# Reordering the first slot, the router and the POOL work of a fused attention + mixture-of-experts kernel

## The chip, the cores and the metric

One core of a Trainium2 chip runs the whole program. The metric is the device time of one execution in microseconds (us). An engine of the core is named as in the profile: PE does the matmuls and transposes, DVE the element-wise vector work, ACT the activation functions, POOL (GpSimd) some element-wise work and all DMAs whose rows are chosen by an index in memory ("indirect"), and SP issues the plain DMAs.

## The reference, cut to what matters

Everything is in 32-bit floats. B = 8 batches, S = 1024 tokens, D = 512; the attention has 16 heads of 32; the experts are E = 8, two per token, 512 to 2048 to 512, at most 160 tokens of a batch per expert.

```python
# attention: no projections; Q, K and V are sines and cosines of scaled inputs
xh = layernorm(x).reshape(B, S, 16, 32)
Q = concat(cos, sin)(xh / (1 + |w_q|) + b_q + t * phi_q)     # K alike
V = cos(.) + sin(.)   of  xh / (1 + |w_v|) + b_v
out = causal_softmax(Q @ K.T / 8) @ V
x = x + cos(.) + sin(.)   of  out / (1 + |w_out|) + b_out
# experts
xn2 = layernorm(x)
p, e = top_k(softmax(xn2 @ Wr + br), 2)
pos = place of the token within its expert, in this batch; kept if pos < 160
y = relu(xn2[rows of e] @ W1[e] + b1[e]) @ W2[e] + b2[e]
x = x + sum over the two experts of p * y
```

## The kernel before, in words

**Attention.** It runs as 32 slots, n = 0 to 31; slot n is batch b = n // 4 and a quarter c = n % 4 of the features (four heads, as two pairs). In a slot PE makes scores (`scores`, matmuls at L680), ACT takes their exponential (L700), PE multiplies by V (`attend`, L714), and PE turns the result (`turn`, through L215). Meanwhile the next slot's angles are made: `qk_pre` has PE transpose the input and DVE form `qk_f` (L521), `angle` makes `qk_r` or `t_r` (L440), ACT squares (L444) and takes sines, `v_pre` and `v_post` (L450) make V. The angle's part t * phi is a table per feature quarter, a "base": `make_base(c)` computes it once and stores it (`base_d`), and later batches load it (`load_base`). Bases 0 and 1 are made at the very start, 2 and 3 in slot 0, base 3 from a POOL iota (L463) through DVE (L471, L491, L225, L226) before `t_r` of the next slot.

**Router.** `router(b)` is a generator that the next batch's slots advance at places written out by hand. The slot c = 0 of batch b + 1 is followed by a "begin" slot (c = 1; the flag `begin`): there DVE makes second-layernorm rows (`rows`, L788), which SP stores to `xn2_d`, PE transposes two of them, DVE copies them out (`xT`, L815, or ACT at L807 for the last batch), PE makes logits (`sums`, L851). Later steps choose the two experts, count the places with PE (L834, from `prior`, L917 to L919), and leave 16 scatters, each of 128 (token, gate) pairs, to a table `slot_d[b]`. POOL issues them in `scatter` (L762); `fetch_slots` (L967) reads the table back to `meta`. `find_rows` (DVE) turns it into row numbers, with which `gather` (POOL DMA, then PE transposes at L215 or L1067) collects an expert's inputs.

**Experts.** For each expert two chunks, of six and four tiles of 128 rows. Both layers are Strassen products, seven matmul products in place of eight, so that weights and inputs have to be mixed (subtracted) first: `mix_w1` (L1095 to L1098, on POOL in the first chunk, else DVE) and `mix_w2` (DVE, L1020 to L1023). Layer 1 is eight steps q of seven products (L1111), layer 2 has a block of seven products (L1156), of eight matmuls each, per pair of tiles; a block ends with `gated` and two `send` (L1178), indirect DMAs that add rows to the output. The last batch's router has no later attention slots; `ending()` advances it, one step per product, through the first chunk's layer 1.

**What sets the order.** PE, DVE, ACT and SP issue in the order in which the program text reaches their instructions. POOL's order is chosen by a scheduler, but where the code pins an instruction. A pool of buffers makes an instruction wait until the former user of its buffer is done; DMAs that write the same table are ordered by waits unless the code says that they are independent.

Of the kernel before, what the change touches and what calls it, by code (L numbers as in the profile page):

```python
# [73 lines left out]
def preln_attn_moe_kernel(  # L74
# [421 lines left out]
    def load_base(n):  # L496
        if n == 2:
            rest(make_base(n))
        if n < NCH:
            return  # L500
        p = qkt.tile([P, 2, S], F32, name="qk_base")
        nc.sync.dma_start(p, base_d[n % NCH])
        bases[n] = p
# [253 lines left out]
    scatters = []  # L757

    def scatter():
        while scatters:  # L760
            b, idx, src = scatters.pop(0)
            nc.gpsimd.indirect_dma_start(  # L762
                out=slot_d[b], out_offset=bass.IndirectOffsetOnAxis(ap=idx, axis=0),
                in_=src, in_offset=None,
            )

    def router(b):
# [9 lines left out]
        for t in range(NTT):  # L777
            nc.vector.bn_aggr(mv[:, t, :], stats[:, t, :, :].rearrange("p c s -> p (c s)"))
        rstd = inverse_root(mv[:, :, 1], "rstd")

# [15 lines left out]

        last = b == B - 1

        def features(g):

            xT = row2.tile([P, NCH, 2 * P], F32, name="xT", bufs=1)
            if last:
                for i, xn in enumerate(ahead):
                    ps = pools["ps_tr"].tile([P, NCH, P], F32, name="ps_t")
                    for c in range(NCH):
                        nc.tensor.transpose(ps[:, c, :], xn[:, c * P : (c + 1) * P], ident)
                    copy(xT[:, :, i * P : (i + 1) * P], ps)  # L807
            else:
                ps = two_banks()
                for i, xn in enumerate(ahead):  # L810
                    for c in range(NCH):
                        at = (NCH * i + c) * 64
                        by_halves(ps[:, :, at : at + 64], xn[:, c * P : (c + 1) * P])
                for a in range(2):
                    copy(  # L815
                        xT.rearrange("p c (i a q) -> p i c a q", a=2, q=64)[:, :, :, a, :],
                        ps[:, a, :].rearrange("p (i c q) -> p i c q", i=2, q=64),
                    )
            if g + 1 < NTT // 2:
                ahead[:] = [rows(2 * g + 2), rows(2 * g + 3)]  # L820
                if not last and 2 * g + 4 == NTT:
                    store()
            return xT

# [42 lines left out]
        for g in range(NTT // 2):  # L867
            xT = features(g)
            yield
            lg = sums(g, xT, lg)  # L870
            yield
# [89 lines left out]
    def fetch_slots(b):  # L961

        rows = slot_d[b][: E * CAP, :].rearrange("(e c) k -> c e k", e=E)
        s0 = b * CAP
        while s0 < (b + 1) * CAP:
            s1 = min((s0 // P + 1) * P, (b + 1) * CAP)
            nc.gpsimd.dma_start(  # L967
                meta[s0 % P : s0 % P + s1 - s0, :, s0 // P, :],
                rows[s0 - b * CAP : s1 - b * CAP],
            )  # L970
            s0 = s1
# [72 lines left out]
    def gather(i):  # L1044

        e, j0, nh = chunks[i]
        xe = pools["xep"].tile([P, NCH, 2, HALF], F32, name="xe")
        for j in range(2 * nh):
            xg = pools["gp"].tile([P, D], F32, name="xg")
            nc.gpsimd.indirect_dma_start(  # L1050
                out=xg, out_offset=None, in_=xn2_d[i % 2],
                in_offset=bass.IndirectOffsetOnAxis(ap=source[:, e, j0 + j, None], axis=0),
            )
            yield None
            dst = xe[:, :, j // nh, j % nh * P : (j % nh + 1) * P]
# [23 lines left out]

    def start(gen, box):  # L1080
        for box[0] in gen:
            yield
# [4 lines left out]
    def mix_w1(i, q):  # L1087
        w = w1_tiles.pop((i, q))
        t = pools["t1p"].tile([P, 4, 2, P], F32, name="t1")
        b11, b12 = w[:, :2, 0, :], w[:, :2, 1, :]  # L1090
        b21, b22 = w[:, 2:, 0, :], w[:, 2:, 1, :]
        t1, t2, t3, t4 = (t[:, k, :, :] for k in range(4))

        mix = nc.gpsimd.tensor_tensor if i == 0 else TT
        mix(t1, b12, b11, ALU.subtract)  # L1095
        mix(t2, b22, t1, ALU.subtract)  # L1096
        mix(t3, b22, b12, ALU.subtract)
        mix(t4, b21, t2, ALU.subtract)  # L1098
        t1_tiles[i, q] = b11, b21, b22, t1, t2, t3, t4
# [47 lines left out]
    def layer2(i, block, hs, aside):  # L1147
# [29 lines left out]
        def send(r):  # L1177
            nc.gpsimd.indirect_dma_start(  # L1178
# [3 lines left out]
            )  # L1182

# [5 lines left out]
        TT(u2, p1, product(5, 4), ALU.add)  # L1189
        TT(u3, u2, product(6, 5), ALU.add)  # L1190
        p5 = product(4, 3)
        TT(u2, u2, p5, ALU.add)
        TT(u2, u2, p3, ALU.add)
        gated(0, 1, u2)
        send(0)
# [16 lines left out]
    def experts_begin():  # L1212

        for name, bufs in (("w1p", 3), ("t1p", 2), ("xep", 1), ("tmp_p", 2), ("gp", 2)):
            pools[name] = to_end.pool(name, bufs, **right)
        find_rows(0)
        for k in range(AHEAD):
            load_ahead(k)
        yield from start(gather(0), first_parts)
        mix_w1(0, 0)  # L1220

    def experts(ending):
        pools["hp"] = to_end.pool("hp", NHQ, **right)
        pools["ps_tr"] = to_end.pool("ps_tr", 2, space=PSUM)
        pools["ps_p"] = to_end.pool("ps_p", 6, space=PSUM)
        box = first_parts
        mixes = loads = iter(())
        for i, (e, j0, nh) in enumerate(chunks):
            parts, box = box[0], [None]
            hs = []  # L1230
            for q in range(NHQ):
                load_ahead(i * NHQ + q + AHEAD)
# [3 lines left out]
                if q > 1:  # L1236
                    next(mixes, None)
                hs.append(layer1(i, q, parts, [ending]))
                if i == 0 and q == NHQ // 2:
                    rest(ending)  # L1240
                    to_router.close()
                    for name, bufs in (("w2p", NHQ), ("yp", 3), ("bp", 1)):
                        pools[name] = to_end.pool(name, bufs, reuse_waits="tile", **left)
                    load_b2(0)
                    rest(load_w2(0))
                elif i == 0 and q == NHQ - 2:
                    mixes = mix_w2(0)
                    next(mixes)
            rest(mixes)
            aside = start(gather(i + 1), box) if i + 1 < len(chunks) else iter(())  # L1250
            for block in range(nh):
                if i == 0 and block == 1:
                    find_rows(1)
                layer2(i, block, hs, aside if i or block else iter(()))
# [24 lines left out]
    load_x(1)  # L1279
    v_post(0, v_st)  # L1280
    magnitude(inv_o)
    rest(base1)
# [3 lines left out]
    place, angles, residual = [None], iter(()), iter(())  # L1286
    for n in range(NCK):
# [5 lines left out]
        pos_n = trig.tile([P, S], F32, name="o_p")  # L1293
        if late:
# [34 lines left out]
        if n == 0:  # L1329
            with_asides(2)  # L1330
        if n == 0 or begin:

            qk_st = rest(qk_pre(n + 1))
            angle(*qk_st)
            angles = keep(place, both(qk_st))
            if n == 0:
                rest(make_base(3))
# [4 lines left out]
        route_on(1)  # L1342
        route_on(1)
# [8 lines left out]
        for g in asides:  # L1352
            rest(g)
        if late:
            turn(1, halves1, pos)
            o_st = o_pre(n - 1, pos)
        route_on(1)
        if n == 2:
            load_b1()
        if c == 3 and b > 0:  # L1360
# [3 lines left out]
            scatter()  # L1364
# [13 lines left out]
        if n == 0:  # L1378
            load_base(2)

# [18 lines left out]
        elif n + 2 < NCK:  # L1399
            qk_st = rest(qk_pre(n + 2))  # L1400
# [3 lines left out]
        route_on(1)  # L1404
# [8 lines left out]
        if more:  # L1413
# [18 lines left out]
    def ending():  # L1432

        o_st = o_pre(NCK - 1, pos_n)
        yield
# [4 lines left out]
        rest(o_post(NCK - 1, o_st))  # L1440
        for _ in range(3):
            yield
        for name in router(B - 1):

            for _ in range(5 if name == "tiles" else 1):
                yield
        fetch_slots(B - 2)
        scatter()
# [34 lines left out]
```

## Time and profile before

| | us |
|---|---|
| median of 3 runs | 3327.51 (3321.74 to 3332.6) |
| the profiled execution | 3319.22 |
| its span, first to last instruction | 3317.5 |
| PE busy | 3195.8 (96%) |
| DVE busy | 2260.7 (68%) |
| ACT busy | 1321.3 (40%) |
| POOL busy | 427.6 (13%) |
| mean granted PE clock | 0.994 |

Attention fills the span from about 40 to 1300 us, some 38.6 us a slot; the experts follow from 1301.7 to about 3306. "Busy" is the time in which an engine works; a share is of the span, over stages of different kinds. A line of the timeline gives the start, the length, the engine, the line of the kernel, the operation with its output and inputs, how many instructions it groups, and in brackets how long the engine sat idle before it and what ended that. A line of the waits gives the engine, the tile and line that waited, what it waited for, and then the total, the number of times and the longest, in us. Releasers are inferred.

### The profile page before, as it was taken

The page shows a single profiled execution, that of the slowest core. Times are in us where ns is not written, and L with a number is a line of the kernel's source. Part 1 is how long each engine was busy: PE and PEld are TensorE (multiplying, and loading weights), DVE is VectorE, ACT ScalarE, POOL GpSimd, SP SyncE. Part 2 cuts the span into 40 slices and gives each one's busy share as a digit, 9 for nine tenths or more (in the row PEclk, how much of TensorE's full clock was granted, in tenths as well). Part 3 has the DMA queues.
Part 4 walks back from the last instruction along what each step waited for, and adds up shares of the span by engine and source line. Part 5 has one row for each costly group of instructions (what it writes and reads, how often), then busy time and mean ns, then how long its engine had stood idle before and what let it go on. Part 6 is the DMA issues. An engine that isn't in the chain of part 4 may idle for free.

```text
span 3317.5 us, 48746 instructions
## 1 busy us (share of the span) xinstructions
PE 3195.8 (96%) x18942; PEld 2166.4 (65%) x18942; DVE 2260.7 (68%) x4953; ACT 1321.3 (40%) x1617; POOL 427.6 (13%) x395
## 2 busy tenths in 40 slices
PE   4999999999999998899999999999999999999998
PEld 2444444444444444588688688688688688688687
DVE  7787888878787675645845845845845845845854
ACT  6888888878787874201201201201201201201201
POOL 2000202021111203321011011011011011011010
PEclk9999999999999999999999999999999999999999
DMA  4445354544535343322322322422322322322321
GB/s 151 124 117 166 97 164 132 152 130 132 179 103 153 92 144 91 112 45 64 118 39 63 117 45 58 119 44 58 120 43 60 118 47 58 117 45 64 111 40 25
DMA packets 235254, 319.74 MB, mean 96 GB/s; under 512 B 22456, under 2 KB 155280, under 8 KB 222992
## 3 DMA queue, kind: packets, MB, share of 16 engines
q1 hardware_dynamic: 211664, 273.38, 27.8%
q0 software_dynamic: 22912, 43.22, 7.3%
q8 instruction: 150, 2.46, 0.3%
q14 instruction: 80, 0.66, 0.1%
q10 hardware_dynamic: 448, 0.02, 0.0%
HBM read 187.62 MB, written 61.82 MB: 75 GB/s over the span
## 4 chain that ended last, share of the span: by engine, by line
PE 56%; DVE 3%; DMA 2%; issue 1%; POOL 0%; ACT 0%; SPq 0%; POOLq 0%; DVEq 0%; ACTq 0%
PE ps_p L1156 28%; PE ps_p L1111 26%; DMA slot_d<-token,slot 1%; PE ps_t L1067 1%; PE ps_s L680 0%; PE av L714 0%; DMA out_dram<-y,slots 0%; DMA xg<-xn_d,source 0%; DVE t L1096 0%; DVE t L1095 0%; ACT hid L1143 0%; DVE hid L1139 0%; DVE u L1137 0%; DVE hid L1140 0%; DVE u L1132 0%
## 5 line engine op out<-in xcount | busy, mean ns | idle before, releaser
L700 ACT ACTIVATE e<-ps_s 128x1024 f32<-128x1024 f32 (+1 forms) x640 | 568.3, 938 | 214.3 <-PE ps_s L680 126.9
L680 PE MATMUL ps_s<-qk 64*128 64x512 f32 (+3 forms) x3072 | 599.5, 507 | 50.6 <-DVE qk_f L521 16.7
L1156 PE MATMUL ps_p<-w,hid 128*128 128x256 f32 x2560 | 569.8, 380 | 0.0
L1156 PEld LDWEIGHTS ps_p<-w,hid 128*128 128x128 f32 x2560 | 484.7, 190 | 66.5
L714 PE MATMUL av<-e,v 128*64 128x512 f32 (+3 forms) x3072 | 524.1, 490 | 0.0
L1156 PE MATMUL ps_p<-w_t,hid 128*128 128x256 f32 x1920 | 430.3, 379 | 0.7 <-DVE w_t L1022 0.7
L680 PEld LDWEIGHTS ps_s<-qk 64*128 64x128 f32 x3072 | 263.0, 189 | 237.4 <-issue 108.6
L1156 PEld LDWEIGHTS ps_p<-w_t,hid 128*128 128x128 f32 x1920 | 361.8, 190 | 48.7 <-DVE w_t L1022 1.1
L714 PEld LDWEIGHTS av<-e,v 128*64 128x64 f32 x3072 | 200.6, 137 | 283.7 <-issue 267.6
L1111 PE MATMUL ps_p<-xe_s,t 128*128 128x256 f32 (+1 forms) x1024 | 299.1, 435 | 7.9 <-POOL t L1096 4.5
L1111 PE MATMUL ps_p<-xe,w 128*128 128x256 f32 (+1 forms) x1024 | 299.9, 436 | 1.4 <-issue 1.1
L1111 PE MATMUL ps_p<-xe,t 128*128 128x256 f32 (+1 forms) x1024 | 296.8, 433 | 0.0
L762 POOL DMA_INDIRECT slot_d<-token,slot x128 | 160.6, 1255 | 1044.7 <-issue 644.3
L1185 ACT COPY p<-ps_p 128x256 f32<-128x256 f32 x40 | 14.7, 368 | 612.1 <-PE ps_p L1156 612.1
L1111 PEld LDWEIGHTS ps_p<-xe_s,t 128*128 128x128 f32 x1024 | 194.1, 190 | 92.5 <-DVE t L1096 7.9
L1111 PEld LDWEIGHTS ps_p<-xe,w 128*128 128x128 f32 x1024 | 193.5, 191 | 84.3 <-DVE hid L1129 5.7
L1111 PEld LDWEIGHTS ps_p<-xe,t 128*128 128x128 f32 x1024 | 194.4, 190 | 80.9 <-issue 0.4
L1050 POOL DMA_INDIRECT xg<-xn_d,source x80 | 78.1, 977 | 1109.3 <-PE ps_t L1067 1024.2
L1178 POOL DMA_INDIRECT out_dram<-y,slots x80 | 126.4, 1580 | 662.3 <-DVE y L1173 522.9
L1126 ACT ACTIVATE p<-ps_p,b_t 128x256 f32<-128x256 f32 (+1 forms) x128 | 65.4, 511 | 329.9 <-DVE y L1172 169.7
L1130 ACT ACTIVATE hid<-hid 128x256 f32<-128x256 f32 (+1 forms) x128 | 60.1, 470 | 321.1 <-DVE hid L1129 321.1
L1143 ACT ACTIVATE hid<-hid,b_more 128x256 f32<-128x256 f32 (+1 forms) x128 | 71.8, 561 | 269.7 <-DVE hid L1142 269.7
(223 smaller groups left out, 3822.7 us busy)
## 6 DMA issues: line engine op xcount, KB each, us to landing
w<-in_L_ffn_W_dram SPq DMA_DIRECT2D x256, 256.0 KB
w<-in_L_ffn_W_dram SPq DMA_DIRECT2D x64, 512.0 KB
qk<-qk_c SPq DMA_DIRECT2D x124, 256.0 KB
qk<-qk_r SPq DMA_DIRECT2D x124, 256.0 KB
qk_base<-base_d SPq DMA_DIRECT2D x28, 1024.0 KB
xn_d<-xn SPq DMA_DIRECT2D x72, 256.0 KB
x_mid<-in_L_attn_x_dram SPq DMA_DIRECT2D x16, 1024.0 KB
out_dram<-x_mid SPq DMA_DIRECT2D x8, 2048.0 KB
```

The costliest lines, as they stand in the source:

```text
L680: nc.tensor.matmul(ps[:, a, at : at + w], lhsT=pair[r, 1, kb * P : (kb + 1) * P], rhs=pair[r, 0, q0 : q0 + w], start=at == 0, stop=not own ...
L700: nc.scalar.activation(e, ps[:, :, :n], AF.Exp, scale=UNIT * UNIT / math.sqrt(2 * DH))
L714: nc.tensor.matmul(av[a * 64 : (a + 1) * 64, q0 - 512 * h :], lhsT=vt[:, kb, 2 * pr + a, :], rhs=es[i][:, a, at : at + w], start=kb == 0, ...
L762: nc.gpsimd.indirect_dma_start(out=slot_d[b], out_offset=bass.IndirectOffsetOnAxis(ap=idx, axis=0), in_=src, in_offset=None,)
L1050: nc.gpsimd.indirect_dma_start(out=xg, out_offset=None, in_=xn2_d[i % 2], in_offset=bass.IndirectOffsetOnAxis(ap=source[:, e, j0 + j, None ...
L1067: nc.tensor.transpose(ps[:, c, :], xg[:, c * P : (c + 1) * P], ident)
L1111: nc.tensor.matmul(ps, lhsT=weights[:, k, :], rhs=rows[:, k, :], start=k == 0, stop=k == 1)
L1126: nc.scalar.activation(p1, product(b11, a11), AF.Identity, bias=b1_t[:, e * NHC + q : e * NHC + q + 1])
L1130: nc.scalar.activation(h11, h11, AF.Relu)
L1143: nc.scalar.activation(h12, h12, AF.Relu, bias=more)
L1156: nc.tensor.matmul(ps, lhsT=hs[k][:, part, cols], rhs=ws[k][weight], start=k == 0, stop=k == NHQ - 1,)
L1178: nc.gpsimd.indirect_dma_start(out=out, out_offset=bass.IndirectOffsetOnAxis(ap=meta[:, e, jj[r], 0:1], axis=0), in_=ys[r], in_offset=None ...
```

## The change

It has seven parts.

1. **First slot.** Base 1 is finished before V of slot 0, base 2 and the small `magnitude(inv_o)` move within slot 0, and base 3 is made in slot 1, not in slot 0.
2. **Begin slots.** On DVE, `v_post` and the next two rows come after `xT` and `qk_f`; later `xT` comes before `qk_f`.
3. **First gathers.** The first chunk's rows are found and four of its gathers issued in slot 30, into buffers of the router, and two more before the first mixtures.
4. **Scatters.** In the last two batches (6 and 7) they no longer wait for each other; half of batch 6's come behind the W1 mixture of q = 2 and the rest after it. The fetch of the slots waits for all scatters of its batch. Other batches stay as they are.
5. **First expert chunk.** The last router's steps come later, its places wait five products; W1's mixtures of q = 6 and 7 go to DVE; W2's mixtures are made 2, 3 and 3 at a time; `find_rows(1)` and the second chunk's gathers come earlier. POOL's order is pinned for the mixtures, the sends of the first chunk and the gathers of chunks 1 and 2.
6. **Layer 2.** Product (4, 3) comes before (6, 5), with it `send(0)`. This holds for all 40 blocks.
7. **Pools** of the expert part wait by tile when a buffer is reused (`reuse_waits="tile"`), and the `gp` pool comes first.

```diff
     def load_base(n):
-        if n == 2:
+        if n < NCH:
             rest(make_base(n))
-        if n < NCH:
             return
...
-    def scatter():
-        while scatters:
+    scattered = {b: [] for b in range(B)}
+    mixed = []
+    def scatter(count=2 * NTT * TOPK, together=False):
+        for _ in range(min(count, len(scatters))):
             b, idx, src = scatters.pop(0)
...
+            if together:
+                tc.add_manual_dep(
+                    ins, mixed[-1].name,
...
+                    reason="behind the mixture",
+                )
+                for other in scattered[b]:
+                    tc.declare_no_dep(ins, other, reason="rows of their own")
+            scattered[b].append(ins)
...
-            if g + 1 < NTT // 2:
-                ahead[:] = [rows(2 * g + 2), rows(2 * g + 3)]
-                if not last and 2 * g + 4 == NTT:
-                    store()
             return xT
+        def next_rows(g):
+            ahead[:] = [rows(2 * g + 2), rows(2 * g + 3)]
+            if not last and 2 * g + 4 == NTT:
+                store()
...
             xT = features(g)
+            if g + 1 < NTT // 2:
+                if not last:
+                    yield
+                next_rows(g)
             yield
...
-            nc.gpsimd.dma_start(
+            ins = nc.gpsimd.dma_start(
...
+            for other in scattered[b]:
+                tc.add_manual_dep(
...
+                    reason="rows of all scatters",
...
     def gather(i):
+        if i == 0:
+            t = row2.tile([P, NCH, 2 * P], F32, name="xT", bufs=1).rearrange("p c t -> p (c t)")
+            places = [row2.tile([P, D], F32, name="xn2") for _ in range(2)]
+            places += [t[:, :D], t[:, D:]]
+            there = [fetch(xg, j) for j, xg in enumerate(places)]
             yield None
+            there += [fetch_next(j) for j in (4, 5)]
...
-        mix = nc.gpsimd.tensor_tensor if i == 0 else TT
...
+        apart = i == 0 and q < 6
+        mix = nc.gpsimd.tensor_tensor if apart else TT
...
         TT(u2, p1, product(5, 4), ALU.add)
+        p5 = product(4, 3)
+        TT(p1, u2, p5, ALU.add)
+        TT(p1, p1, p3, ALU.add)
+        gated(0, 1, p1)
+        send(0)
         TT(u3, u2, product(6, 5), ALU.add)
-        p5 = product(4, 3)
-        TT(u2, u2, p5, ALU.add)
-        TT(u2, u2, p3, ALU.add)
-        gated(0, 1, u2)
-        send(0)
...
-        for name, bufs in (("w1p", 3), ("t1p", 2), ("xep", 1), ("tmp_p", 2), ("gp", 2)):
-            pools[name] = to_end.pool(name, bufs, **right)
-        find_rows(0)
+        for name, bufs in (("gp", 2), ("w1p", 3), ("t1p", 2), ("xep", 1), ("tmp_p", 2)):
+            pools[name] = to_end.pool(name, bufs, reuse_waits="tile", **right)
...
-        pools["ps_tr"] = to_end.pool("ps_tr", 2, space=PSUM)
-        pools["ps_p"] = to_end.pool("ps_p", 6, space=PSUM)
+        pools["ps_tr"] = to_end.pool("ps_tr", 2, space=PSUM, reuse_waits="tile")
+        pools["ps_p"] = to_end.pool("ps_p", 6, space=PSUM, reuse_waits="tile")
...
                 if q > 1:
-                    next(mixes, None)
+                    for _ in range(1 if i else 3):
+                        next(mixes, None)
...
                     mixes = mix_w2(0)
-                    next(mixes)
+                    for _ in range(2):
+                        next(mixes)
+            if i == 0:
+                find_rows(1)
             rest(mixes)
             aside = start(gather(i + 1), box) if i + 1 < len(chunks) else iter(())
+            if i == 0:
+                aside = behind(2, aside)
             for block in range(nh):
-                if i == 0 and block == 1:
-                    find_rows(1)
-                layer2(i, block, hs, aside if i or block else iter(()))
+                layer2(i, block, hs, aside)
...
-    v_post(0, v_st)
-    magnitude(inv_o)
-    rest(base1)
+    rest(base1)
+    v_post(0, v_st)
...
+        if n == NCK - 2:
+            find_rows(0)
+            next(first_gather)
...
             qk_st = rest(qk_pre(n + 1))
+            if begin:
+                v_post(n, v_st)
+                next(route)
             angle(*qk_st)
             angles = keep(place, both(qk_st))
-            if n == 0:
-                rest(make_base(3))
...
+        if n == 0:
+            load_base(2)
+            magnitude(inv_o)
...
-            scatter()
+            if b < B - 1:
+                scatter()
...
     def ending():
         o_st = o_pre(NCK - 1, pos_n)
+        scatter(NTT * TOPK // 2, together=True)
         yield
...
         for name in router(B - 1):
-            for _ in range(5 if name == "tiles" else 1):
+            if name == "tiles":
+                scatter(together=True)
+            for _ in range({"tiles": 6, "places": 5}.get(name, 1)):
                 yield
         fetch_slots(B - 2)
-        scatter()
+        scatter(together=True)
         fetch_slots(B - 1)
```

## The prediction

> **What bounds it now.** I read the page, then TensorE (PE) busy by stage, PE's waits, the timeline around each, and the chain of waits. PE is busy 3195.8 of 3317.5 us, so about 122 us are to be had. Windows (start:end, length, PE, PE weight loads, VectorE = DVE, ScalarE = ACT, GpSimd = POOL, clock, DMA share, GB/s):
>
> ```profile
> 0.00:40.00 40.00, 7.91 (x44) 4.86 (x46) 34.60 (x74) 26.21 (x28) 22.30 (x52) 1.00 0.60 171
> 40.00:80.00 40.00, 24.89 (x166) 12.14 (x163) 23.69 (x24) 24.03 (x24) 1.84 (x1) 0.83 0.42 135
> 160.00:1300.00 1140.00, 1102.44 (x9674) 544.03 (x9670) 886.44 (x1784) 923.12 (x932) 160.04 (x137) 1.00 0.46 133
> 1300.00:1400.00 100.00, 86.22 (x318) 50.88 (x319) 69.20 (x173) 27.20 (x48) 36.54 (x44) 0.97 0.40 124
> 1600.00:3200.00 1600.00, 1597.32 (x6769) 1260.28 (x6768) 1007.83 (x2352) 219.44 (x442) 161.90 (x126) 1.00 0.28 72
> ```
>
> The experts, half the time, lose 2.7 us in 1600 and DVE works 63% of it: nothing to win there. The loss sits at the start (15 us in 40–80), in the attention and in the first expert chunk (14 us in 1300–1400). PE's waits name it:
>
> ```profile
> PE ps_s L680 <- DVE qk_f L521: 16.7, 8, 4.0
> PE ps_s L680 <- ACT e L700: 13.5, 5, 10.9
> PE ps_s L851 <- DVE xT L815: 6.6, 8, 0.8
> PE ps_s L680 <- DVE xT L815: 4.5, 6, 0.9
> PE ps_p L1111 <- POOL t L1096: 4.5, 2, 3.7
> PE ps_t L1067 <- DMA xg<-xn_d,source: 3.6, 1, 3.6
> PE ps_t L834 <- DVE prior L917: 3.5, 1, 3.5
> ```
>
> The timelines give the places: the 10.9 us wait and what DVE does before it, one begin slot (the slot that starts a router), the tail.
>
> ```profile
> 53.32 1.54 DVE L471 TENSOR_SCALAR x_mid<-x_mid,vecs 128x1024 f32<-128x1024 f32 x2 [4.84 <-POOL x_mid L463]
> 47.27 4.27 PE L680 MATMUL ps_s<-qk 64*128 64x512 f32 x12 [4.01 <-DVE qk_f L521]
> 62.52 1.86 PE L680 MATMUL ps_s<-qk 64*128 64x384 f32 x6 [10.88 <-ACT e L700]
> 394.69 1.14 PE L680 MATMUL ps_s<-qk 64*128 64x384 f32 x8 [0.86 <-DVE xT L815]
> 399.13 1.99 PE L680 MATMUL ps_s<-qk 64*128 64x512 f32 x8 [2.62 <-DVE qk_f L521]
> 3309.85 1.55 POOL L1178 DMA_INDIRECT out_dram<-y,slots  x1 [4.00 <-DMA out_dram<-y,slots]
> ```
>
> The chain shows the scatters, each waiting until the one before has landed, with W1's mixture behind them:
>
> ```profile
> 1320.79 4.06 DMA slot_d<-token,slot
> 1325.11 4.69 DMA slot_d<-token,slot
> 1330.85 0.83 POOL slots L967
> 1331.70 0.74 POOL t L1095
> ...
> 1333.83 2.93 PE ps_p L1111 x4
> ```
>
> **What the skill says.** "DMA: Bandwidth & Descriptors", section "Anatomy of one DMA — SWDGE (gpsimd) path": about 2.0 us per DMA are fixed, nearly all completion latency. The trace agrees (shortest scatter landing 2.1 us, median 3.1), and POOL is busy only 0.96 us per scatter, so waiting, not issuing, is what side by side removes. The same page, "Two DMAs through the same engine are not ordered": only the completion semaphore orders them; so the slot fetch must wait for all 16. "TensorE: Matmul & The Clock Gate", "What's actually happening": after an idle window of some 3.4 us the array runs at half speed for about as long. Here twelve matmuls took 4.27 us after 4.01 idle, eight 2.06 just before it, and 40–80 was granted 0.83; so a long wait costs more than its length. "GPSIMD Engine Reference", "Specifications": POOL shares SBUF interfaces with two-input DVE instructions; L1144 took 1.76 us at 1391.7 against 0.56, with a POOL mixture beside it.
>
> **Part 1, first slot.** Before, slot 0's DVE runs v_post and base 1's tail, then qk_f (44.5), waits 4.84 us for POOL's iota, builds base 3 (1.54+1.23+1.23+2.29 = 6.29 us), and only then makes t_r at 59.6, which ACT's square (60.4) and three exponentials ahead of PE's 62.5 stand behind. After, base 3 is built in slot 1 and qk_f comes first: qk_f at 40.6 (2.72) and qk_r (1.23) end at 44.6; ACT's squares and absolutes (2.19+1.99) run to 48.7, v_p's and t_r's DVE work (1.28+1.22+0.69) meanwhile, v_p's square (1.15) to 49.8. So the exponentials start at about 49.8 instead of 61.5: 11.7 us, the 4.01 us wait at qk_f being inside it; a 2.64 us wait at 82.5 for o_p goes too, 14.3. But base 3's 6.29 us now stand before slot 1's t_r, ready about 3.3 us after ACT wants it; with ACT's slack about 2.65 is given back. Net about **11.7** (7 if both moved bases stall slot 1; 15 with none and the clock back). SP's queue gets the base stores before and after the qk sends in another order; the 1 MB stores delay nothing that is due within 20 us.
>
> **Part 2, begin slots (seven).** The waits sum to 26.0 us: 0.5–0.9 at xT, 1.6–2.6 at qk_f, 0.8 at the second xT. The diff puts av_sb, xT, qk_f ahead of v_post (1.21) and of the two rows (1.06, plus 0.55–0.83 waiting for xn2's store). So qk_f ends about 3.1 us earlier, and that wait goes. But v_post and rows still have to be done before the second xT, and DVE is without a pause from the first rows to it: 13.7–14.0 us before, 13.05 after, only the store wait being saved. What PE wins at qk_f it mostly waits for at the logits (L851). I take 1.0 per slot, +0.4 at the second xT: 1.4 × 7 = **10** (20 if PE has other work there; 26 would be all; 5 if v_post, now later, delays the next attend).
>
> **Part 3, gathers ahead (slot 31).** Waits of 2.76 (put down to the first mixture on POOL, which gathers queue with) and 0.69+1.88 (gathers): 5.3. Four gathers are issued a slot earlier (landing 3.4 us against 38.6 us), two more before the mixtures. Their price on POOL, 6 × 0.98, moves, it isn't added; queued behind them are batch 6's scatters. With about 1.2 us of half clock: **6.5** (4–8).
>
> **Part 4, chunk 0.** From 1301.7 to the end of its layer 2 PE works 154.6 us at full clock and takes 178: 23.5 lost. Before: 3.67 (mixture behind 16 chained scatters, 1278–1329), 1.69+1.90 (router's rows and copies), 3.52+0.93 (prior), 0.85, 0.69, 3.57 (chunk 1's gather behind batch 7's chain, 1366.7–1418.9 = 52 us), about 5 at half clock. After: 8 of batch 6's scatters stand before W1 mixture 2 (of q=2) and 8 behind it, at 0.96+0.3 each 20 us for a batch; mixture 3 is ready 32.6 us after the start, wanted at 39. The router begins two products later and waits five for its places, so the prior's stall is covered; but DVE has 52 us of work up to q=4's end, a bubble of 2.9 at the start, and 3.4 of waits on ACT: I take 57±2 us against PE's ideal 52.6 and 69.8 before: 13. W2's mixtures at 2+3+3 in q=6 and 7 take away 0.69, the earlier find_rows and gathers 3.57 and 1.7 of clock; against it 2.1 as DVE runs three mixtures (5.4 us) before (0,7)'s results, and 0.8 for a gather behind send(0). Batch 7's slots land 29.5 us after q=4, find_rows is reached at 34: if they are late, DVE, in order, stops, and layer 2 with it. Sum **18** (10–23.5). The fetch's new wait on all scatters has only POOL's mixtures and scatters behind it.
>
> **Part 5.** (4,3) before (6,5) brings send(0) forward by one product, 3.46 us. Elsewhere hidden; in the last block send(1), ready at 3307.0, starts at 3309.85 because send(0) lands late: it would start at 3307.3, **2.5** (0–3). Chunk 2's last gather is pinned behind a send: **−0.8**. Pools that wait by tile: nothing; the stage has 2.7 us of waits in all, and if a bank's release became later that is the rival below.
>
> Sum 11.7+10+6.5+18+2.5−0.8 = 47.9. The profiled execution took 3319.22 (span 3317.5 and 1.7 around it); 3271.3 after, a ratio of 0.9856. The median of the runs, 3327.51, is 0.25% above that execution; the ratio on it gives **3279.5**.
>
> **Rivals.** (a) Everything named goes: 15+20+8+23.5+3 = 69.5, 3258. For it: PE's order is untouched, and every removed wait has a late engine with time elsewhere (DVE 68%). Against: DVE's unbroken 13 us in the begin slots. (b) Given back: DVE is the limit there and in chunk 0's router (69.2 of 100 busy, with PE waiting on it at L806 and L834); lower ends 7+5+4+10+0−0.8 = 25, 3302. (c) Slower: in layer 2's new order DVE's last reading of (4,3) still waits for (6,5), now the later product, so (4,3)'s bank is held one product longer; with six banks there are five others to go on. If PE had to wait for it once a block, up to 3.46 us × 40 blocks = 138 us; at 1.2 us a block (47.9/40) the gain is gone, above it the kernel is slower: at 2 us, 3359. Against it: DVE at 63%, and its adds of 0.42 us each follow within a product. (d) The scatters side by side don't help: if landings under W2's and the output's traffic stretch (one took 8.2 us), chunk 0 keeps its 18: 3297, within (b).
>
> **How the numbers follow.** Forecast 0.62, (a) 0.13, (b) with (d) 0.18, nothing within 0.3% (10 us, about what a measurement can tell from no change) 0.03, (c) 0.04. Range 3256 to 3304: from (a) to (b), all but some 0.15. Forecast's own: 3268 to 3292. Faster 0.93, same 0.03, slower 0.04.
>
> **What would show it.** Part 1: the x6 at 62.52 comes 11 us earlier, and 80–120 has about as much PE time as before. Part 2: L680's wait on qk_f falls from 16.7 to under 3, L851's on xT rises from 6.6 to over 10. Part 3: no L215 wait on xg. Part 4: L1111 no longer waits on L1095/L1096, 1300–1400 shows over 92 busy, scatters of the last two batches stand under 1.4 us apart. Part 5: send(1) issued within 0.5 us of its data. Wrong if 1600–3200 shows over 10 us idle, or find_rows stalls DVE for microseconds.

## The result and the profile after

The changed kernel takes 3285.68 us (median of 4 runs, 3283.79 to 3287.43), the kernel before 3325.78 (4 runs, 3321.74 to 3332.6): a ratio of 0.9881 with a 95% interval of 0.9865 to 0.9897. The forecast was 3279.5 with a range of 3256 to 3304. The profiled execution of the changed kernel took 3283.79, with a span of 3282.1, so between the two profiled executions the gain is 35.4 us, where 47.9 had been summed up.

PE by stage, in the columns of the prediction. The stages are now at other places of the program, so only the first and the long one compare directly: 40 to 80 gained 8.9 us of PE time, 1600 to 3200 is as full as it was. The part numbers from here on are those of the prediction: its part 4 takes in parts 4 and 5 of the change, its part 5 is the change's parts 6 and 7 and the pinned gathers of chunk 2.

```profile
40.00:80.00 40.00, 33.83 (x249) 17.05 (x247) 26.27 (x30) 30.91 (x31) 2.13 (x1) 0.91 0.53 162
160.00:1300.00 1140.00, 1113.42 (x9682) 552.57 (x9680) 898.33 (x1826) 923.86 (x936) 169.47 (x148) 1.00 0.47 133
1300.00:1400.00 100.00, 92.68 (x376) 63.70 (x373) 70.92 (x172) 19.46 (x36) 34.08 (x37) 0.95 0.41 108
1600.00:3200.00 1600.00, 1596.74 (x6814) 1269.14 (x6813) 998.35 (x2355) 218.02 (x442) 165.16 (x128) 1.00 0.29 72
```

PE's waits of the changed kernel (total, times, longest). Against the list before: L680's wait on qk_f, now L679, fell from 16.7 to 3.9, and the waits for POOL's mixtures and for DVE's prior all but went. New in this size are small waits at lg and prob, and one of 4.7 us at the first matmul of layer 2 (L1214).

```profile
PE ps_s L679 <- ACT e L699: 10.5, 4, 5.9
PE ps_s L869 <- DVE xT L832: 5.5, 7, 0.8
PE ps_p L1214 <- DVE hid L1187: 4.7, 1, 4.7
PE ps_s L679 <- DVE prob L876: 4.0, 7, 0.6
PE ps_s L679 <- DVE qk_f L520: 3.9, 7, 0.6
PE ps_s L852 <- DVE lg L874: 3.5, 7, 0.6
PE ps_t L1117 <- DMA xg<-xn_d,source: 3.3, 2, 1.8
```

To see where the time went, take the start of the same matmul in both traces: the first score of a slot, the first layer-1 matmul of a step, and so on. Both kernels reach these places in the same sequence, so the difference at each is the gain so far.

| PE reaches | before, us | after, us | gain | gain of the stretch | predicted |
|---|---|---|---|---|---|
| slot 3 | 166.08 | 155.53 | 10.55 | 10.55 | 11.7 (part 1) |
| slot 30 | 1214.30 | 1193.98 | 20.32 | 9.77 | 10 (part 2) |
| layer 1, chunk 0 | 1301.69 | 1273.49 | 28.21 | 7.89 | 6.5 (part 3) |
| chunk 0, step q = 5 | 1371.46 | 1334.71 | 36.75 | 8.54 | 13 (of part 4) |
| layer 2, chunk 0, third block | 1456.18 | 1420.81 | 35.37 | -1.38 | 5 (rest of part 4; its terms add up to 3.1) |
| layer 1, chunk 2 | 1580.82 | 1547.50 | 33.32 | -2.05 | -0.8 |
| last matmul of layer 2 | 3305.34 | 3272.49 | 32.84 | -0.48 | 0 |
| end | 3317.5 | 3282.06 | 35.44 | 2.60 | 2.5 (part 5) |

Parts 1 to 3 and the tail came near to what was summed. That parts 1 to 3 give exactly the 28.2 forecast for them together is luck: they were off by -1.2, -0.2 and +1.4. The first chunk gave 7.2 instead of 18. These are its places in the changed kernel's timeline, with those of the first slots and of one begin slot:

```profile
52.31 2.08 PE L679 MATMUL ps_s<-qk 64*128 64x384 f32 x8 [5.93 <-ACT e L699]
93.12 1.14 PE L679 MATMUL ps_s<-qk 64*128 64x384 f32 x8 [2.88 <-ACT e L699]
385.26 1.99 PE L679 MATMUL ps_s<-qk 64*128 64x512 f32 x8 [0.56 <-DVE qk_f L520]
392.19 0.31 PE L852 MATMUL ps_s<-gather_e,lg 128*32 128x8 f32 x16 [0.57 <-DVE lg L874]
393.29 0.64 PE L869 MATMUL ps_s<-xT,wr_sb 128*32 128x256 f32 x8 [0.79 <-DVE xT L832]
1299.23 0.87 PE L869 MATMUL ps_t<-xT,wr_sb 128*32 128x256 f32 x8 [2.66 <-ACT xT L824]
1366.73 8.49 PE L1214 MATMUL ps_p<-w,hid 128*128 128x256 f32 x28 [4.66 <-DVE hid L1187]
1396.17 0.63 PE L1117 MATMUL ps_t<-ident,xg 128*128 128x128 f32 x4 [1.50 <-DMA xg<-xn_d,source]
```

The line at 1366.73 is the most expensive. DVE's timeline ahead of it shows why: after the last result of q = 6 five of W2's mixtures, of four instructions each, run one behind the other from 1357.57 to 1366.1, and only then the first result of q = 7 is read. PE's next product waits until then for a free bank, a part of the memory that it writes results to.

```profile
1357.09 0.56 DVE L1202 TENSOR_TENSOR hid<-hid 128x384 f32<-128x384 f32 x1 [0.68 <-ACT hid L1201]
1357.57 0.42 DVE L1050 TENSOR_TENSOR w_t<-w 128x256 f32<-128x256 f32 x1
...
1365.79 0.43 DVE L1053 TENSOR_TENSOR w_t<-w,w_t 128x256 f32<-128x256 f32 x1
1366.13 0.55 DVE L1187 TENSOR_TENSOR hid<-p,ps_p 128x384 f32<-128x384 f32 x1
```

### The profile page after: what moved, and what is told of

It reads as the page before. It is cut to its first block, busy times and chain, and to the rows that moved or that the text cites. A ratio compares the mean times of both kernels' runs of the same rounds, so it can differ in the third digit from the quotient of the medians.

```text
span 3282.1 us, 48761 instructions
## 1 busy us (share of the span) xinstructions
PE 3191.8 (97%) x18942; PEld 2166.0 (66%) x18942; DVE 2252.1 (69%) x4961; ACT 1322.4 (40%) x1617; POOL 421.3 (13%) x387
## 4 chain that ended last, share of the span: by engine, by line
PE 73%; DVE 6%; issue 3%; ACT 1%; DMA 1%; SPq 0%; POOL 0%; POOLq 0%; DVEq 0%; ACTq 0%
PE ps_p L1214 28%; PE ps_p L1169 25%; PE av L713 9%; PE ps_s L679 8%; ACT e L699 1%; PE ps_t L1117 1%; PE ps_s L215 1%; DVE qk_f L520 1%; PE ps_s L693 1%; DVE t L1153 1%; DMA xg<-xn_d,source 1%; DVE qk_r L450 0%; DMA xn_d<-xn 0%; DVE xT L832 0%; DMA qk<-qk_r 0%
## 5 line engine op out<-in xcount | busy, mean ns | idle before, releaser
L679 PE MATMUL ps_s<-qk 64*128 64x512 f32 (+3 forms) x3072 | 596.5, 505 | 32.8 <-DMA qk<-qk_r 12.4
L1214 PE MATMUL ps_p<-w,hid 128*128 128x256 f32 x2560 | 570.3, 380 | 4.7 <-DVE hid L1187 4.7
L1214 PEld LDWEIGHTS ps_p<-w,hid 128*128 128x128 f32 x2560 | 485.0, 191 | 71.6 <-DVE hid L1187 5.3
L1214 PE MATMUL ps_p<-w_t,hid 128*128 128x256 f32 x1920 | 428.9, 379 | 0.0
L679 PEld LDWEIGHTS ps_s<-qk 64*128 64x128 f32 x3072 | 262.4, 188 | 219.1 <-issue 106.9
L1214 PEld LDWEIGHTS ps_p<-w_t,hid 128*128 128x128 f32 x1920 | 362.0, 190 | 47.6
```

The source lines that it names most:

```text
L679: nc.tensor.matmul(ps[:, a, at : at + w], lhsT=pair[r, 1, kb * P : (kb + 1) * P], rhs=pair[r, 0, q0 : q0 + w], start=at == 0, stop=not own ...
L1214: nc.tensor.matmul(ps, lhsT=hs[k][:, part, cols], rhs=ws[k][weight], start=k == 0, stop=k == NHQ - 1,)
```

## The experiments

Each kernel is timed against the kernel before on the same chip; the changed kernel's own ratio, taken again in the second set, is 0.9888 (0.9871 to 0.9905). A ratio says what a whole kernel is worth; which stretch an edit moved is read from the trace, as in the table above. The changed kernel's two traces differ by 0.6 us in the first expert chunk and by up to 1.0 elsewhere, so less than that is no difference. Each set of four ran on one chip, the three sets on three different chips.

### W2's mixtures at 1, 1 and 6 again

```diff
-                    for _ in range(1 if i else 3):
-                        next(mixes, None)
+                    next(mixes, None)
...
-                    for _ in range(2):
-                        next(mixes)
+                    next(mixes)
```

> The changed kernel with W2's mixtures of the first chunk at 1, 1 and 6 again instead of 2, 3 and 3. Theory A (DVE is the limit at the switch from layer 1 to layer 2, so their place only decides where PE waits): the 4.7 us wait for a PSUM bank at the first layer-2 product goes and that product starts about 7 us earlier, but the fourth product, the first that needs all mixtures, waits some 6 to 8 us for six mixtures behind the row finding; its start and the end of the kernel move by less than 3 us. Theory B (the five mixtures in front of the last layer-1 results are themselves the loss): 5 to 7 us faster.

3294.79 us, 0.9906 (0.9877 to 0.9935). From the start of layer 1 to the third block of layer 2 it took 144.2 us (1283.85 to 1428.03), the changed kernel 147.3 (1273.49 to 1420.81). This stretch is "the first chunk" in what follows. Of the 3.2 us less, 0.9 come before q = 5, where the two are the same. The whole isn't faster, because slots 30 and 31 took 8.6 us longer here; that is taken up with the changed kernel's second run. The wait of 4.7 us is gone, and the one that theory A had put at the fourth product came out as 0.27:

```profile
1372.66 2.59 PE L1169 MATMUL ps_p<-xe_s,w 128*128 128x384 f32 x4 [2.43 <-ACT p L1184]
1389.56 0.70 PE L1214 MATMUL ps_p<-w_t,hid 128*128 128x256 f32 x2 [0.27 <-DVE w_t L1052]
```

The wait of 2.43 isn't the edit's. It stands on ACT's copy of a product that PE had finished long before; ACT had been idle for 5.5 us. The same wait, of 2.40 and 1.72 us, is in the next kernel and in the one with two mixtures on POOL, which ran on the same chip, and in no trace of another chip. The two kernels at the end of this section have the mixtures at the same places without it. From q = 7 to the fourth product of layer 2 they took 19.4 us, this one 23.8, the changed kernel 26.5 and 26.0 in its two traces. So up to the fourth product the five mixtures in front cost 6.6 to 7.1 us, as theory B has it. But at the third block only 1.6 to 3.8 us of that are left in those two kernels: PE then waits for the last mixtures and the gathers, as theory A has it. Each theory has a half of it.

### The 2 MB store behind the last router's logits

```diff
-        if b == B - 1:
-            store()
...
+        if last:
+            store()
         yield "choice"
```

> The changed kernel with the 2 MB store of the last batch's rows to the output issued after the last router's logits instead of before its statistics. Theory A (the store fills the DMA queues between 1284 and 1304 us, so the router's row stores land late, DVE waits 7.1 us for their buffers, and PE stands behind DVE): DVE's waits for the row stores fall below 2 us, the scatters of batch 6 land in 3 to 5 us instead of 7 to 12, q = 5 of the first chunk starts 3 to 5 us earlier, and 2 to 4 us are left at the end. Theory B (the delay comes from W1's loads or from the number of scatters): waits and times as in the changed kernel, within 1 us.

3297.13 us, 0.9904 (0.9874 to 0.9933). DVE's waits of 7.1 us for the row stores are gone, as theory A has it, but from the start of layer 1 to q = 5 PE took 60.0 us, against 61.2 in the changed kernel and 60.3 and 61.1 in the two kernels of this set that are the same up to there. DVE now waits for PE's transposes (3.8 us) and for the logits (3.3) instead. In the version with four edits (below), on another chip, the same move brought nothing either (61.7). The first links of theory A hold, the last doesn't: PE had not stood behind those waits of DVE.

### The scatters of the last two batches one behind the other

```diff
-                for other in scattered[b]:
+                for other in []:
                     tc.declare_no_dep(ins, other, reason="rows of their own")
```

> The changed kernel with the scatters of batches 6 and 7 waiting for each other again, everything else as changed. Theory A (scatters side by side are what frees POOL): batch 6's second eight take 30 to 50 us, W1's mixture (0,3) is late by 10 us or more and batch 7's slots by 25 or more, DVE stands at the row finding; 20 to 40 us slower than the changed kernel, all of it in the first chunk. Theory B (landings, not issues, set the pace and the fetch waits for all of them anyway): under 5 us slower.

3310.6 us (8 runs), 0.995 (0.9935 to 0.9964). Batch 6's second eight take 31 us, against 10.4 in the changed kernel, and batch 7's sixteen, up to the fetch behind them, 52 (1346.9 to 1399.2, POOL's timeline) against 26.4. PE stands for 16 us at the first product that needs all of W2's mixtures, because DVE had stood for 23 us at the row finding, until the slots were there:

```profile
1324.49 2.85 PE L1169 MATMUL ps_p<-xe_s,t 128*128 128x384 f32 x8 [1.94 <-POOL t L1153]
1402.69 0.18 DVE L1069 TENSOR_SCALAR source<-slots 128x32 int32<-128x32 int32 x1 [23.35 <-DMA slots<-slot_d]
1404.17 1.22 PE L1214 MATMUL ps_p<-w_t,hid 128*128 128x256 f32 x2 [16.32 <-DVE w_t L1052]
```

The first chunk is 20 us longer than in the changed kernel. Theory A holds, at its lower end: the mixture came 1.9 us late, not 10, the slots as late as expected.

### Two of W2's mixtures on POOL

```diff
+            mix = nc.gpsimd.tensor_tensor if e == 0 and k in (2, 3) else TT
-            TT(t[:, 1, :], b12, b22, ALU.subtract)
+            mix(t[:, 1, :], b12, b22, ALU.subtract)
...
```

> The changed kernel with two of W2's eight mixtures of the first chunk (k = 2 and 3) on POOL, which is idle then, instead of DVE. Theory A (DVE's 8.6 us of mixtures in front of the last layer-1 results is what PE waits for): DVE is free 3.7 us earlier, the 4.7 us wait shrinks to about 1, the half clock behind it goes, 3 to 6 us faster. Theory B (PE waits for the slots or the gathers): no change, or 1 to 2 us slower since the gathers stand behind POOL's mixtures.

3293.81 us, 0.9897 (0.987 to 0.9925). The first chunk took 146.8 us, as long as the changed kernel's two (147.3 and 146.8). The wait of 4.7 us shrank to 0.24 and PE reached the fourth product 4.1 to 4.6 us sooner after q = 7, but this was given back at the next step: POOL made the mixtures only behind its fetch of the slots (1381 to 1386.8), and DVE's row finding, 0.17 us elsewhere, took 3.92 and ended with POOL's last subtraction:

```profile
1382.94 3.92 DVE L1070 TENSOR_SCALAR source<-slots 128x32 int32<-128x32 int32 x1 [0.79 <-DMA slots<-slot_d]
1386.78 0.41 DVE L1051 TENSOR_TENSOR w_t<-w 128x256 f32<-128x256 f32 x1
```

That the mixtures on DVE are what PE waits for is confirmed, theory A's gain is not.

### The changed kernel again

> The changed kernel itself, unaltered, beside the three others, because the runs that should have equalled it up to the last attention slot lost 3 to 4 us in slot 30 (where six gathers are issued one after the other) and up to 6 in slot 31 (where eight scatters are), and in slot 31 and at q = 7 an engine started late although what it waits for was done. Theory A (such a row of indirect DMAs holds up the other engines' signals in some placements, by chance of chip or run): the changed kernel shows these losses too in some executions, 3283 to 3300 us. Theory B (the edits did it): 3282 to 3288 us, no loss in slots 30 and 31.

3283.49 us, 0.9888 (0.9871 to 0.9905), and within 1.1 us of its first trace at every place of the table. On this chip theory B's numbers hold. But the four kernels above have the same instructions in slots 30 and 31, and there they took 38.3 to 40.0 us for slot 30 against 35.9 in the ten others traced, the kernel before among them; and three of the four took 49.5 to 50.5 for slot 31, where the changed kernel and the others that leave that slot as it is took 43.6 (one of them 44.8). The one that did not lose slot 31 is the one with chained scatters; it doesn't have the wait of 1.7 to 2.4 us at q = 7 either. In slot 31 of the kernel with mixtures at 1, 1 and 6, DVE's reciprocal started 5.9 us after the transposes it reads, with nothing on DVE, 1.7 us after POOL had issued the last of eight scatters. The edits are not the cause, at least of two of the four: the version with four edits has the mixtures at 1, 1 and 6 and the late store together, and on its chip it lost nothing in these slots. All four ran on the same chip, so chip and chance can't be told apart here: that a row of indirect DMAs delays other engines' signals on some chips is a guess that fits, and it stays open.

### No V product in the begin slots

```diff
             if begin:
-                v_post(n, v_st)
                 next(route)
```

> The changed kernel without V's last multiplication (1.21 us on DVE) in the seven begin slots; V of those slots is left as it was, so this part of the result is not computed. Theory A (DVE's unbroken work from the rows to the second xT sets these slots): PE's waits on lg, xT and prob there, 1.9 us together, shrink and each begin slot is 0.8 to 1.3 us shorter, 6 to 9 us in all. Theory B (PE's waits there come from its own order or from DMAs): under 2 us in all.

This kernel leaves out V's last multiplication in the seven begin slots. 3277.8 us, 0.9872 (0.9855 to 0.989). From slot 5 to slot 30 it gained 18.16 us on the kernel before where the changed kernel, on the same chip, gained 10.48 in that stretch: 7.7 us for seven slots, 1.1 each of the 1.21 taken out. In the begin slot shown above, the waits at lg and xT of 0.57 and 0.79 became one of 0.34:

```profile
384.24 1.99 PE L679 MATMUL ps_s<-qk 64*128 64x512 f32 x8 [0.56 <-DVE qk_f L520]
391.19 0.64 PE L869 MATMUL ps_s<-xT,wr_sb 128*32 128x256 f32 x8 [0.34 <-DVE xT L832]
```

Theory A: DVE's chain sets these slots.

### All gathers in slot 31 again

```diff
-        if n == NCK - 2:
-            find_rows(0)
-            next(first_gather)
...
+        find_rows(0)
+        yield from start(first_gather, first_parts)
```

> The changed kernel with all six first gathers issued in slot 31 again, through two buffers. Theory A (the gathers were late, as part 3 of the prediction has it): slot 31 is 5 to 9 us longer with PE's waits on the gathered rows back, slot 30 at its usual 35.9 us. Theory B (the gain of 7.9 us in slot 31 came from the scatters that no longer stand before the first mixtures): under 3 us.

3286.88 us, 0.9899 (0.9881 to 0.9916). Slot 31 took 47.26 us: 3.6 more than with the gathers ahead (43.6), 4.3 less than before (51.51). PE's waits on gathered rows are back:

```profile
1233.24 0.47 PE L215 MATMUL ps_s<-ident,xg 64*128 64x64 f32 x8 [1.72 <-DMA xg<-xn_d,source]
1237.56 0.46 PE L215 MATMUL ps_s<-ident,xg 64*128 64x64 f32 x8 [1.43 <-DMA xg<-xn_d,source]
```

It lies between the theories: 3.6 of part 3's 7.9 us are the gathers ahead. For the other 4.3 the traces show what is gone here too: a wait of 2.8 us put down to POOL's first mixture, one of 1.1 in front of layer 1's first matmul, and 3.4 us at half of the PE clock. Which edit took these away, the order of POOL's first mixtures and scatters or another, was not tried.

### The first slot as before

```diff
-    rest(base1)
-    v_post(0, v_st)
+    v_post(0, v_st)
+    magnitude(inv_o)
+    rest(base1)
...
+            if n == 0:
+                rest(make_base(3))
```

> The changed kernel with the first slot as before (V of slot 0 and the small vector work ahead of base 1, base 3 made in slot 0). Theory A (part 1's working: the exponentials wait behind base 3's DVE work): the 10.9 us wait at about 62.5 us is back, slot 3 starts 9.5 to 11 us later and so does everything after it. Theory B (the wait is for POOL's iota or the first loads and stays wherever base 3 is made): under 4 us.

3294.81 us, 0.9919 (0.9902 to 0.9935). Slot 3 starts at 166.12, as before the change (166.08), and the old waits are back. With the first slot as changed it starts at 155.5 in the first trace, and at 155.7 and 156.8 in the two other kernels of this set that have it, so part 1 is worth 9.3 to 10.6 us:

```profile
47.28 5.33 PE L680 MATMUL ps_s<-qk 64*128 64x512 f32 x12 [4.67 <-DVE qk_f L521]
62.71 2.08 PE L680 MATMUL ps_s<-qk 64*128 64x384 f32 x8 [10.01 <-ACT e L700]
```

### The begin slots' DVE order as before

```diff
-            if begin:
-                v_post(n, v_st)
-                next(route)
...
-        if more and not begin:
+        if more:
             v_post(n + 1, v_st)
```

> The changed kernel with DVE's order in the seven begin slots as before. Theory A (DVE's chain to the second xT is shorter only by the wait for the row store): each begin slot is 0.9 to 1.6 us longer, one or two of them 2 to 3 through the half clock, 8 to 11 us in all. Theory B (the waits at qk_f were wholly saved): 2 to 3 us each, 15 us or more.

3294.3 us, 0.9922 (0.9906 to 0.9939). Between slots 3 and 30 it gained 1.2 us on the kernel before instead of 9.8, so the order is worth 8.6 us, or some 9 against the two other kernels of this set that leave these slots as they are. Theory A's range holds. The waits of before are back (0.53, 2.54 and 0.83 us in the same slot).

### Layer 2's products in the old order

```diff
-        p5 = product(4, 3)
-        TT(p1, u2, p5, ALU.add)
...
         TT(u3, u2, product(6, 5), ALU.add)
+        p5 = product(4, 3)
```

> The changed kernel with layer 2's products (6,5) and (4,3) in the old order. Theory A (only the last block's second send waits for the first): the kernel's last 2.6 us are back and nothing else moves. Theory B (the new order costs a bank somewhere, or gains in every block): the chunks between move by 1 us or more each.

3283.45 us, 0.9888 (0.9871 to 0.9904), the same as the changed kernel. From the last matmul to the end it takes 12.16 us again, 2.6 more than the changed kernel, as theory A has it. But from the fourth product of its first chunk to the third block it is 1.7 us shorter, and in chunk 1's layer 2 2.0: the new order loses there at least what it brings at the end. The chunks behind these two don't move. POOL's timeline shows how, first of the changed kernel, then of this one: the send, now a product earlier, stands in front of the fourth gather, which then waits for the send's data as well.

```profile
1383.70 0.95 POOL L1078 DMA_INDIRECT xg<-xn_d,source  x1 [8.34 <-PE ps_t L1117]
1389.96 1.64 POOL L1236 DMA_INDIRECT out_dram<-y,slots  x1 [5.31 <-DVE y L1231]
1391.91 0.99 POOL L1078 DMA_INDIRECT xg<-xn_d,source  x1 [0.30 <-issue]
```

```profile
1383.36 0.94 POOL L1078 DMA_INDIRECT xg<-xn_d,source  x1 [7.85 <-PE ps_t L1117]
1387.26 0.94 POOL L1078 DMA_INDIRECT xg<-xn_d,source  x1 [2.95 <-PE ps_t L1117]
1393.52 1.64 POOL L1236 DMA_INDIRECT out_dram<-y,slots  x1 [5.32 <-DVE y L1231]
```

### Two versions with what the runs pointed to

The first has the mixtures at 1, 1 and 6, the row finding behind them, chunk 1's gathers two products later, chunk 2's gathers not pinned, and the late store; the second has the early store and makes base 3 in slot 1 only after that slot's angles.

```diff
-            if i == 0:
-                find_rows(1)
             rest(mixes)
+            if i == 0:
+                find_rows(1)
...
-                aside = behind(2, aside)
+                aside = behind(4, aside)
...
-            if i in (1, 2):
+            if i == 1:
                 tc.keep_in_program_order(ins)
```

> The changed kernel with four edits in the first two chunks: W2's mixtures at 1, 1 and 6, the row finding after them and the second chunk's gathers two products later; the 2 MB store after the last router's logits; chunk 2's gathers no longer pinned. Theory A (DVE is the limit from the router to layer 2's fourth product, so only the waits that are not DVE's go): 4 to 6 us faster than the changed kernel, 2 of them in chunk 1's layer 2, 2 to 4 in chunk 0. Theory B (the order chosen by the change is already the best): no change or slower.

3277.0 us, 0.9867 (0.985 to 0.9884), 6.5 us under the changed kernel on the same chip. The first chunk is 3.2 us shorter, chunk 1's layer 2 is back at the 51.0 us of the kernel before (52.9 in the changed kernel). The layer switch now runs without idle time up to the fourth product, where the mixtures come 1.7 us late in two pieces.

```diff
-        if n == 0:
-            load_base(2)
+        if n < 2:
+            load_base(n + 2)
...
-            if n + 3 < NCK:
+            if n and n + 3 < NCK:
                 load_base(n + 3)
```

> The changed kernel with W2's mixtures at 1, 1 and 6, the row finding after them and the second chunk's gathers two products later, chunk 2's gathers no longer pinned, the store where the change has it, and base 3 made after the next slot's angles in slot 1. Theory A (base 3's 6.3 us in front of slot 1's t_r cost PE the 2.9 us wait at 93 us): that wait goes, 2 to 3 us more than the version that has the other edits alone, 7 to 9 us faster than the changed kernel. Theory B (base 3 is then late for slot 3's angles): the wait moves to slot 2 or 3 and nothing is gained.

3276.61 us (3272.88 to 3277.58), 0.9862 (0.9845 to 0.9878), the fastest here. The 2.9 us wait at 93 is gone and slot 3 starts at 154.13; with base 3 where the change has it, it starts between 155.3 and 157.5. A part of the gain comes back as a wait of 1.05 at 104.6. Theory A, at its lower end: against the version before it, on another chip, the whole differs by less than the runs can tell.

## Why the prediction was right, and where it was off

**Part 1** was right with its working. The exponentials start at 51.25, not 49.8, because qk_r had a wait of 1.5 us on a DMA that the sum did not have; what base 3 gives back in slot 1 is 2.88 (2.65 had been written). Predicted 11.7, measured 10.55, and 9.3 to 10.6 by undoing it.

**Part 2** was right in size and in cause: 10 predicted, 9.77 measured, 8.6 to 9.1 by undoing it, and the leave-out shows that DVE's chain is the limit. The wait on qk_f fell to 3.9, not under 3. Where PE waits instead was called wrongly: L851's wait on xT did not rise from 6.6 to over 10 but fell to 5.5, and what was given back stands at lg and prob (3.5 and 4.0).

**Part 3**: 6.5 predicted, 7.89 measured; only 3.6 of it is the gathers' own, so the size is right and the cause only half shown.

**Part 4** was mis-sized: 18 in the sum, 7.2 measured. The shortfall of 10.8 has four pieces.
- The terms that the prediction writes down for it add up to 16.1, not 18 (13 + 0.69 + 3.57 + 1.7 - 2.1 - 0.8). Nothing stands behind the other 1.9.
- From the start of layer 1 to q = 5 "57±2 us" was taken and 61.2 measured: the gain is 4.5 short of the 13. By PE's gaps and the granted clock, the 69.8 us before are 11.7 idle, 3.4 lost to half clock (stretches with a granted PE clock of 0.5) and 54.7 of work; the 61.2 after are 4.8, 1.7 and 54.7. PE's ideal had been put at 52.6, which is 2.1 too low; the rest is idle time and half clock, of which the largest piece is the 2.66 us on ACT's copy of xT. The row stores were not the cause (the late store).
- "2.1 as DVE runs three mixtures (5.4 us)" is the worst term. Five mixtures stand there, the two at the end of q = 6 as well as the three at the start of q = 7, 8.6 us, and the idle time brings the half clock that the prediction itself had quoted for such waits. PE waits 4.66 us and reaches the fourth product 6.6 to 7.1 us later than in the two kernels without a wait there. Against the kernel before, from q = 5 to the fourth product, it lost 6.1 where 2.1 was forecast, 4.0 too much. The change list had the numbers 2, 3 and 3 in it; the error was to look only at the three inside q = 7. Not all of it could have been had by placing them better, as the first experiment shows.
- From the fourth product to the third block 4.7 of 5.2 came. The gather behind send(0) cost 1.7, not 0.8, and chunk 2's 2.05, not 0.8: not the send's issue alone is added to the gather, but the wait for the send's data on DVE.

The direction of part 4 was right: the chained scatters cost 20 us in the first chunk. Of its signs, PE's waits on POOL's mixtures are gone and the row finding did not stall DVE. PE is over 92 us busy in 1300 to 1400 too, but that window holds another stretch of the program by now.

**Part 5** was right at the tail (2.5 predicted, 2.6 measured). With the gathers' 3.7 us the new order of layer 2 gains nothing, where the sum had 2.5 less 0.8 and 0.8. The pools that wait by tile were not undone alone; 1600 to 3200, as full as before, shows no effect of them.

The sum for the profiled execution was thus 12.5 us too high. The medians moved by 40.1, 4.7 more than the profiles, since the profiled execution of before lay 6.6 under its median and that of after 1.9. So a part of the 12.5 is hidden in the medians by chance; in the second set, on one chip, the medians moved by 35.4 like the profiles. Of the rivals, (b) came nearest in the first chunk (10, with 7.2 measured) and was wrong in the rest, (c) never came: 1596.7 of 1600 us are busy in 1600 to 3200. (d) is refuted by the chained scatters, though the landings did stretch, up to 12 us. That PE's order is untouched, said for rival (a), isn't so: in the traces the first chunk's gathered rows are turned at other places of slot 31, the last router's matmuls stand later among chunk 0's products, and two products change places in every block of layer 2.

## What to carry to other kernels

When work of an in-order engine is spread over an earlier stage, count all of it that stands ahead of the result the next engine waits for, not only what is issued in the step itself, and add what the half clock behind the idle time costs. Then look at what the engine has to do next: here 2.8 to 5 of the 6.6 us that better placing gained were lost again a few products later. A pinned DMA behind another costs the time until the first one's data is ready, not its issue. Where an engine works almost without a gap, as DVE does in the begin slots, reordering gains only a part of what others wait for it (9.8 of 26 us here), and work taken off the engine gains nearly its full length (7.7 of 8.5 us).

## What the runs showed of the hardware that was not expected

- A row finding on DVE of 0.17 us took 3.92 and ended within 0.1 us of POOL's last subtraction (two mixtures on POOL). The Trainium skill, "GPSIMD Engine Reference", section "Specifications", has the shared SBUF interfaces as the place where the two meet, for DVE instructions with two SBUF inputs or in a 2-port mode. The row finding has one input; in which mode it ran no run here shows. By the trace it stood for the rest of POOL's series, not for one instruction of it.
- Side by side, a scatter that lands in 2.1 to 3.1 us alone took 6.8 to 12.0 while the 2 MB store and W1's loads filled the DMA engines (mean share 0.91 from 1284 to 1304 us). With that store later (the version with four edits, share 0.42) the same eight took 2.1 to 6.4. The eight of slot 31, side by side with no such store, took 2.1 to 2.9. So it is mostly the store, not the number of scatters, that stretches them.
- The same wait of 2.65 us of PE, in front of the last router's logits, was followed within 1 us by 3.4 to 6.8 us at half clock in seven of the thirteen traces of changed kernels, and not in the six others.
- Slots 30 and 31, with the same instructions, took 2.4 to 4.1 and up to 6.8 us longer on one chip than on the others, with engines starting late and no wait to show for it. It is open why.
